# A graph layer in fp32 on one core: edge-part adds two units behind TensorE, first-layer evictions on ScalarE, a longer ring of gathered rows

## The chip, the cores and the metric

The kernel runs on one core of a Trainium2 chip. The metric is the device time of one execution in microseconds (us), the median of three runs: 2553.75 us before the change (2550.78 to 2557.36). About 0.3% is what repeated runs of this kernel can tell from no change.

TensorE (PE in the profile) multiplies matrices into PSUM; VectorE (DVE) and ScalarE (ACT) read PSUM and work on SBUF; GpSimd (POOL) here issues the gathers; SyncE (SP) issues most other transfers. Each of the engines works through its own instructions in program order and waits for the others by semaphores.

## The reference, cut to what matters

There are 6250 nodes with 256 features, and 206250 edges sorted by destination, each with a polarity and 64 raw features.

```python
h = relu(layernorm(x))
e = relu(raw @ W_e1.T + b_e1) @ W_e2.T + b_e2        # first and second layer, per edge
edge_emb = (e * (polarity + 0.01)) @ W_le.T + b_le
msg = relu(h[src] + edge_emb)
aggr = segment_sum(msg, dst)                          # sums over the edges of a node
n = layernorm((h + aggr) @ W_g1.T + b_g1) * ln_g + ln_b
out = x + relu(n) @ W_g2.T + b_g2
```

## The kernel before

**Tiling.** Edges are cut into 403 blocks of 512 (a block is four tiles of 128 edges). A *unit* is half a block, 256 edges; there are 806. A *pair* is two blocks, that is four units; its raw features come in one load (`load_pair`, line 232). W_e2 and W_le are multiplied together once (line 383), so that an edge needs two matrix products: the *first layer* (line 237) and the *edge part* (line 264). Six blocks make a *group*, whose sums gather in a PSUM accumulator.

**The steps of one unit and pair.**
- `first_layer(q)`, for a pair: four matmuls (line 248) into four PSUM buffers, then four evictions with bias and relu into `e1`: three by ScalarE (line 257) and the fourth by VectorE (line 254).
- `edge_part(u)`: four matmuls (line 272) of `e1` with the joint matrix into one PSUM buffer `pz`, then one VectorE add of the bias row, `msg = pz + bc_s` (line 277), which empties the buffer. (ScalarE copies a few of the first 22 instead, line 275.)
- gather: GpSimd fetches the 256 rows `h[src]` by two indirect DMAs (line 537) into `hg`, a ring of HG = 16 units.
- `whole(u)`: two VectorE operations (line 584) make `hg = msg * polarity + hg`, then ScalarE applies relu in place (line 589).
- `add_up(b)`: sixteen-fold narrow matmuls (line 601) sum the rows of a block into the group's accumulator by a selection matrix that VectorE builds (line 566).
- The nodes of 128-wide windows are finished in steps spread over later units (`finish_nodes`, line 148, and `node_work`, line 649); VectorE's parts that read TensorE's results are at lines 175, 197 and 703.

**What sets the order.** The order is written out by hand: the program runs in the order in which Python issues it (`manual_schedule`), each engine in its own queue. The main loop (line 750) runs over units. `forward(u)` issues the edge part; when u % 4 is 1 it calls `turn_of`. For pairs 6 to 195 (`by_two`), a *turn* comes every eight units and issues two first layers with the sums between them (lines 298 to 302). There are 95 such turns. After `forward`, the loop issues a piece of selection or node work, then `whole` for units that lie a distance behind (line 758): 22 units at first, one less every 36 units, at least LEAST = 1. Then it issues a node step that is due (not in the loop's passes 0 and 1 of eight).

**Buffers.** `pz`, the first layer's results and the nodes' products share one rotation of seven PSUM buffers (line 224); the eighth holds the group accumulators. A buffer is reused by the seventh allocation after its own, as soon as its reader is done. Gathers are issued in step with TensorE and never further ahead than HG units past the last sums (line 553).

Of the kernel before, what the change touches and what calls it, by code (L numbers as in the profile page):

```python
# [9 lines left out]
F32 = mybir.dt.float32  # L10
I32 = mybir.dt.int32
AF = mybir.ActivationFunctionType
# [5 lines left out]
P = 128  # L18
N = 6250
D = 256  # L20
# [16 lines left out]
NP = -(-NB // 2)  # L37
MARGIN = 768
DEG = E // N
LEAD = 22  # L40
LEAST = 1
# [1 line left out]
STEP = 1.282  # L43
AFLOAT = 6.0
SHRINK = 36
HG = 16
FEW = 6
QUIET = (0, 1)
TURN = 1
# [47 lines left out]
def gnn_kernel(ctx: ExitStack, tc: tile.TileContext, x, src_c, dst_c, dst_r, pol_c, raw_t, w_e1t, w_e2,  # L97
               w_let, w_g1t, w_g2t, vec_c, row_v, x_t, out):
    nc = tc.nc
# [20 lines left out]
    bc_s = const.tile([P, 2, D], F32, name="bc_s")  # L120
# [96 lines left out]
    with fast:  # L217
# [19 lines left out]
        def first_layer(q):  # L237

            bs = [b for b in (2 * q, 2 * q + 1) if b < NB]
            if not bs:  # L240
                return
            for b in bs:
                e1[b] = e1_p.tile([P, 2, 512], F32, name="e1")
            pe = {}
            for c in range(2):
                for s, b in enumerate(bs):
                    pe[s, c] = ps().rearrange("p a b -> p (a b)")
                    z = nc.tensor.matmul(pe[s, c], we1_s[s * F:(s + 1) * F, c * P:(c + 1) * P],  # L248
                                         raw[q][s * F:(s + 1) * F, :], start=True, stop=True)
                paced(LAYER, z)  # L250
            for c in range(2):
                for s, b in enumerate(bs):
                    if s == c == 1:
                        nc.vector.tensor_scalar(e1[b][:, c, :], pe[s, c], be1_s[:, c:c + 1], 0.0, op0=ALU.add,  # L254
                                                op1=ALU.max)
                    else:
                        nc.scalar.activation(e1[b][:, c, :], pe[s, c], AF.Relu, bias=be1_s[:, c:c + 1])  # L257
            raw.pop(q)

        def plain(u):  # L260

            return u < LEAD and u % 3 == 1

        def edge_part(u):

            nonlocal last_z
            b, v = divmod(u, 2)
            pz = ps()
            for i in range(2):
                k = (2 * v + i) * P  # L270
                for c in range(2):
                    last_z = nc.tensor.matmul(pz[:, i, :], e1[b][:, c, k:k + P], wc_s[:, c, :], start=c == 0, stop=c == 1)  # L272
            msg[u] = msg_p.tile([P, 2, D], F32, name="msg")
            if plain(u):
                nc.scalar.activation(msg[u], pz, AF.Copy)
            else:
                nc.vector.tensor_add(msg[u], pz, bc_s)  # L277
            if v == 1:
                e1.pop(b)
            paced(EDGE, last_z)  # L280

        last_z = None
        sums = lambda last: None
        paced = lambda us, behind: None

        def by_two(q):
            return FEW <= q < NP - FEW

        def turn_of(q):


            if not by_two(q):
                if q + 2 < NP:
                    first_layer(q + 2)
                sums(q == NP - 1)
                load_pair(q + 4)
            elif q % 2 == 0:
                first_layer(q + 2)
                sums(False)
                first_layer(q + 3)  # L300
                load_pair(q + 4)
                load_pair(q + 5)
# [39 lines left out]
        with tc.tile_pool(name="p1", bufs=4) as p1, tc.tile_pool(name="p1x", bufs=11) as p1x:  # L342
# [76 lines left out]
            for k in range(len(parts) + 1):  # L419
# [15 lines left out]
                for _ in range((k > 0) + (k > 2 and k % 3 > 0)):  # L435
                    u = next(units, None)
# [85 lines left out]
        with tc.tile_pool(name="hg", bufs=HG) as hg_p, tc.tile_pool(name="ms", bufs=5) as ms_p, \  # L522
# [227 lines left out]
            for u in range(LEAD, NU):  # L750
# [219 lines left out]
```

## Time and profile before

| | |
|---|---|
| median of 3 runs | 2553.75 us |
| the profiled execution | 2558.52 us |
| its span, first to last instruction | 2556.8 us |
| mean granted TensorE clock | 0.965 |
| TensorE busy | 2378.9 us, 93% |
| VectorE busy | 1647.0 us, 64% |
| ScalarE busy | 980.9 us, 38% |
| GpSimd busy | 1638.7 us, 64% |

The profile is of one execution. Busy time counts an engine's own work, not its waits. A row of a group has the line, engine, operation, what it writes and reads with its shape, and the count; after the first bar its busy time in us and the mean of one in ns; after the second the idle time of the engine just in front of those instructions, with what ended most of it. The chain of work that ended last goes back from the last instruction, at each step to whatever released it. A timeline row has start and duration in us, and in brackets the idle time before it. Ends of matmuls are modelled. PE is TensorE's matmuls, PEld its weight loads. A stretch's row has the length, then the busy time of PE, PEld, DVE, ACT and POOL with counts, then the granted clock, the DMA share and GB/s.

### The profile page before, as it was taken

How to read it: one execution, taken by the hardware profiler on the slowest of the kernel's cores; microseconds unless marked ns; L12 is line 12 of the kernel's file. 1: busy time of each engine (PE TensorE's matmuls, PEld its weight loads, DVE VectorE, ACT ScalarE, POOL GpSimd, SP SyncE). 2: the span in 40 equal slices, each digit the busy share in tenths (PEclk: the TensorE clock that was granted, in tenths of full speed). 3: DMA queues.
4: the chain of work that ended last, by engine and by line, in shares of the span. 5: the costliest groups of instructions: out<-in, count | busy, mean ns of one | idle time of the engine just before them, and what ended most of it. 6: DMA issues, size and time to landing. Idle time of an engine off the chain costs nothing.

```text
span 2556.8 us, 35901 instructions
## 1 busy us (share of the span) xinstructions
PE 2378.9 (93%) x12382; PEld 1670.3 (65%) x12382; DVE 1647.0 (64%) x3953; ACT 980.9 (38%) x1701; POOL 1638.7 (64%) x1675
## 2 busy tenths in 40 slices
PE   9998998999999989999999999999999999899987
PEld 7666666666666757666666666666666666666664
DVE  7776666666666666666656666656666666656655
ACT  7333333343343433334333433433333433333432
POOL 5666666666666666666666666666666665666662
PEclk9999999999999999998999999999999999999998
DMA  8433343334334433433343444334334333343341
GB/s 300 129 115 113 108 134 112 114 114 130 113 108 125 130 119 106 133 108 117 111 144 101 115 126 122 110 106 137 112 114 131 118 107 114 109 131 109 119 119 55
DMA packets 156084, 309.24 MB, mean 121 GB/s; under 512 B 33183, under 2 KB 77944, under 8 KB 155896
## 3 DMA queue, kind: packets, MB, share of 16 engines
q0 software_dynamic: 77376, 211.39, 28.5%
q1 hardware_dynamic: 77364, 92.23, 11.4%
q10 hardware_dynamic: 1156, 3.28, 0.3%
q8 instruction: 98, 1.61, 0.3%
q14 instruction: 90, 0.74, 0.1%
HBM read 293.92 MB, written 12.85 MB: 120 GB/s over the span
## 4 chain that ended last, share of the span: by engine, by line
PE 82%; issue 5%; DVE 5%; another core or an unknown queue 3%; ACT 1%; DVEq 0%; ACTq 0%
PE pz L272 49%; PE pz L248 17%; PE pd L601 9%; PE pz L701 3%; DVE hg L584 2%; PE pz L195 2%; PE pz L169 2%; DVE msg L277 1%; ACT e L257 0%; DVE sel L566 0%; PE pz L185 0%; ACT hg L589 0%; DVE hT L676 0%; DVE e L254 0%
## 5 line engine op out<-in xcount | busy, mean ns | idle before, releaser
L537 POOL DMA_INDIRECT hg<-hb_d,src_s x1612 | 1601.5, 993 | 861.2 <-issue 525.4
L272 PE MATMUL pz<-wc_s,e 128*128 128x256 f32 x6448 | 1486.5, 384 | 51.8 <-issue 38.6
L272 PEld LDWEIGHTS pz<-wc_s,e 128*128 128x128 f32 x6448 | 1216.7, 192 | 318.8 <-issue 99.8
L589 ACT ACTIVATE hg<-hg 128x512 f32<-128x512 f32 x805 | 508.5, 632 | 1117.2 <-DVE hg L584 854.1
L277 DVE TENSOR_TENSOR msg<-pz,bc_s 128x512 f32<-128x512 f32 x799 | 546.6, 686 | 325.1 <-PE pz L272 152.3
L584 DVE SCALAR_TENSOR_TENSOR hg<-msg,pol_s,hg 128x256 f32<-128x256 f32 x1612 | 697.5, 480 | 2.6 <-issue 1.5
L248 PE MATMUL pz<-raw,we_s 64*128 64x512 f32 x1612 | 510.3, 653 | 42.8 <-issue 22.9
L254 DVE TENSOR_SCALAR e<-pz,vecs 128x512 f32<-128x512 f32 x201 | 150.5, 749 | 500.0 <-PE pz L248 201.4
L257 ACT ACTIVATE e<-pz,vecs 128x512 f32<-128x512 f32 x605 | 376.4, 686 | 225.1 <-PE pz L248 84.9
L248 PEld LDWEIGHTS pz<-raw,we_s 64*128 64x128 f32 x1612 | 177.2, 195 | 281.6 <-issue 164.7
L601 PE MATMUL pd<-hg,sel 128*32 128x256 f32 x3216 | 258.6, 408 | 53.1 <-issue 50.9
L601 PEld LDWEIGHTS pd<-hg,sel 128*32 128x32 f32 x3216 | 114.0, 115 | 221.2 <-issue 170.0
L566 DVE SCALAR_TENSOR_TENSOR sel<-iota_w,zero_c,rel 128x128 f32<-128x128 f32 x403 | 138.8, 344 | 0.0
L613 ACT ACTIVATE ms<-pd 128x256 f32<-128x256 f32 x66 | 25.5, 386 | 191.7 <-remote 60.1
L701 PEld LDWEIGHTS pz<-s,ms 128*128 128x128 f32 x548 | 70.3, 194 | 9.1 <-issue 3.8
L701 PE MATMUL pz<-s,ms 128*128 128x128 f32 x548 | 71.7, 278 | 4.7 <-issue 2.5
L676 DVE SCALAR_TENSOR_TENSOR hT<-hT,zero_c,stb 128x128 f32<-128x128 f32 (+1 forms) x196 | 67.2, 343 | 1.7 <-issue 1.7
L169 PE MATMUL pz<-wg_s,hT 128*128 128x256 f32 (+1 forms) x196 | 52.8, 389 | 9.9 <-DVE hT L703 7.4
L195 PE MATMUL pz<-wg_s,nT 128*128 128x256 f32 (+1 forms) x196 | 53.9, 393 | 5.6 <-ACT hg L589 2.7
L169 PEld LDWEIGHTS pz<-wg_s,hT 128*128 128x128 f32 (+1 forms) x196 | 36.5, 191 | 20.0 <-DVE hT L703 9.7
L379 POOL TENSOR_TENSOR hb<-xt,rows_b 128x256 f32<-128x256 f32 (+1 forms) x49 | 34.2, 729 | 23.4 <-DMA xt<-in_x_dram 12.7
L195 PEld LDWEIGHTS pz<-wg_s,nT 128*128 128x128 f32 (+1 forms) x196 | 37.7, 195 | 15.2 <-issue 6.4
(91 smaller groups left out, 393.0 us busy)
## 6 DMA issues: line engine op xcount, KB each, us to landing
raw<-in_raw_t_dram SPq DMA_DIRECT2D x202, 256.0 KB
hg<-hb_d,src_s POOLq DMA_INDIRECT x1612
stb<-st_d SPq DMA_DIRECT2D x49, 128.0 KB
hb_d<-hb SPq DMA_DIRECT2D x12, 512.0 KB
xt<-in_x_dram SPq DMA_DIRECT2D x48, 128.0 KB
hT<-in_x_t_dram SPq DMA_DIRECT2D x48, 128.0 KB
out_dram<-ot SPq DMA_DIRECT2D x48, 128.0 KB
xt<-in_x_dram SPq DMA_DIRECT2D x11, 512.0 KB
```

Source lines behind the costliest of these rows:

```text
L169: nc.tensor.matmul(ph[:n, 0, :], aT[:, c, :n], wg1_s[:, c, :], start=c == 0 and not bias_by_pe, stop=c == 1)
L195: nc.tensor.matmul(po[:n, 0, :], nT[:, c, :n], wg2_s[:, c, :], start=c == 0, stop=c == 1)
L248: z = nc.tensor.matmul(pe[s, c], we1_s[s * F:(s + 1) * F, c * P:(c + 1) * P], raw[q][s * F:(s + 1) * F, :], start=True, stop=True)
L254: nc.vector.tensor_scalar(e1[b][:, c, :], pe[s, c], be1_s[:, c:c + 1], 0.0, op0=ALU.add, op1=ALU.max)
L257: nc.scalar.activation(e1[b][:, c, :], pe[s, c], AF.Relu, bias=be1_s[:, c:c + 1])
L272: last_z = nc.tensor.matmul(pz[:, i, :], e1[b][:, c, k:k + P], wc_s[:, c, :], start=c == 0, stop=c == 1)
L277: nc.vector.tensor_add(msg[u], pz, bc_s)
L537: g = nc.gpsimd.indirect_dma_start(out=hg[u][:, i, :], out_offset=None, in_=hb_d, in_offset=bass.IndirectOffsetOnAxis(ap=src_s[:, 2 * u + ...
L584: nc.vector.scalar_tensor_tensor(hg[u][:, i, :], m[:, i, :], pol_s[:, 2 * u + i:2 * u + i + 1], hg[u][:, i, :], op0=ALU.mult, op1=ALU.add)
L589: nc.scalar.activation(hg[u], hg[u], AF.Relu)
L601: z = nc.tensor.matmul(acc[g][j * W:(j + 1) * W, :], sel[g][:, k * S + j, :], m[:, j % 2, :], start=k == 0, stop=b == blocks_of(g)[-1])
L701: nc.tensor.matmul(pa[:, c, :n], ms[g][:, c * P:(c + 1) * P], box["sel2"][i][:, :n], start=i == 0, stop=i == len(gs) - 1)
```

## The change

- For the pairs 6 to 195 all four evictions of a first layer go to ScalarE (line 257); line 254 is left for the pairs at the start and the end.
- Between those pairs the add of a unit is no longer issued with its matmuls. `edge_part` puts the buffer into `parts_of`; the new function `added(behind)` issues adds until only `behind` are left. The loop calls `added(2)` after `whole`, and the turn calls `added(0)` after the sums, ahead of the second first layer. Elsewhere the add still follows its unit.
- The least distance of `whole` is 3 units instead of 1 between those pairs.
- HG is 20 instead of 16.
- The memory that the program reserves in each SBUF partition for the descriptors of GpSimd's DMAs is set to 8192 bytes; without the argument it is 16384. Four units of `hg` take 8192 bytes of a partition.

The instructions of TensorE, GpSimd and SyncE keep their order. ScalarE has 190 more and VectorE 190 fewer.

```diff
-HG = 16
+HG = 20
+BEHIND = 2
...
-                    if s == c == 1:
+                    if s == c == 1 and not (FEW <= q < NP - FEW):
                         nc.vector.tensor_scalar(e1[b][:, c, :], pe[s, c], be1_s[:, c:c + 1], 0.0, op0=ALU.add,
                                                 op1=ALU.max)
                     else:
...
-            msg[u] = msg_p.tile([P, 2, D], F32, name="msg")
-            if plain(u):
-                nc.scalar.activation(msg[u], pz, AF.Copy)
-            else:
-                nc.vector.tensor_add(msg[u], pz, bc_s)
+            parts_of[u] = pz
             if v == 1:
                 e1.pop(b)
             paced(EDGE, last_z)
+            if not by_two(u // 4):
+                added(0)
+
+        def added(behind):
+
+            while len(parts_of) > behind:
+                u = next(iter(parts_of))
+                pz = parts_of.pop(u)
+                msg[u] = msg_p.tile([P, 2, D], F32, name="msg")
+                if plain(u):
+                    nc.scalar.activation(msg[u], pz, AF.Copy)
+                else:
+                    nc.vector.tensor_add(msg[u], pz, bc_s)
...
             elif q % 2 == 0:
                 first_layer(q + 2)
                 sums(False)
+                added(0)
                 first_layer(q + 3)
...
                 piece()
-                while made < u + 1 - max(LEAST, LEAD - u // SHRINK) - (by_two(u // 4) and (u + 1) % 8 == TURN):
+                least = LEAST + BEHIND * by_two(u // 4)
+                while made < u + 1 - max(least, LEAD - u // SHRINK) - (by_two(u // 4) and (u + 1) % 8 == TURN):
                     gathers(made + 1)
                     whole(made)
                     made += 1
+                added(BEHIND)
                 due()
...
-    nc = bacc.Bacc("TRN2", target_bir_lowering=False, num_devices=1)
+    nc = bacc.Bacc("TRN2", target_bir_lowering=False, num_devices=1, dynamic_dma_scratch_size=8192)
```

More of the change, by code (lines that the diff above doesn't have):

```diff
@@ L280, in edge_part @@
             paced(EDGE, last_z)
+            if not by_two(u // 4):
[9 more added lines that the diff above has]
+                    nc.vector.tensor_add(msg[u], pz, bc_s)
+        parts_of = {}
         last_z = None
```

## The prediction

> **What bounds the kernel now.** The page comes first: its head, the chain of work that ended last (by engine), and the groups.
>
> ```profile
> span 2556.8 us, 35901 instructions
> ...
> PE 2378.9 (93%) x12382; PEld 1670.3 (65%) x12382; DVE 1647.0 (64%) x3953; ACT 980.9 (38%) x1701; POOL 1638.7 (64%) x1675
> ...
> PE 82%; issue 5%; DVE 5%; another core or an unknown queue 3%; ACT 1%; DVEq 0%; ACTq 0%
> ...
> L537 POOL DMA_INDIRECT hg<-hb_d,src_s x1612 | 1601.5, 993 | 861.2 <-issue 525.4
> L272 PE MATMUL pz<-wc_s,e 128*128 128x256 f32 x6448 | 1486.5, 384 | 51.8 <-issue 38.6
> ...
> L589 ACT ACTIVATE hg<-hg 128x512 f32<-128x512 f32 x805 | 508.5, 632 | 1117.2 <-DVE hg L584 854.1
> L277 DVE TENSOR_TENSOR msg<-pz,bc_s 128x512 f32<-128x512 f32 x799 | 546.6, 686 | 325.1 <-PE pz L272 152.3
> L584 DVE SCALAR_TENSOR_TENSOR hg<-msg,pol_s,hg 128x256 f32<-128x256 f32 x1612 | 697.5, 480 | 2.6 <-issue 1.5
> ...
> L254 DVE TENSOR_SCALAR e<-pz,vecs 128x512 f32<-128x512 f32 x201 | 150.5, 749 | 500.0 <-PE pz L248 201.4
> L257 ACT ACTIVATE e<-pz,vecs 128x512 f32<-128x512 f32 x605 | 376.4, 686 | 225.1 <-PE pz L248 84.9
> ```
>
> TensorE is the bound: 93% busy, 82% of the chain. What it does not hold of the chain is what a reordering can win. VectorE is busy only 64%, yet it idles 325.1 us in front of the add L277 and 500.0 us in front of the eviction L254, both waiting for TensorE. It works in program order, so whatever stands behind such a wait is late, although the engine has time. TensorE then waits for two things that VectorE feeds: the rows L584 (through L589) that the sums L601 read, and the PSUM buffers that L277 empties.
>
> Where in the run does this cost? The chain of waits, taken in four stretches (shares of each stretch):
>
> ```profile
> by line: PE pz L272 48.1%; PE pz L248 15.0%; PE pd L601 7.4%; issue 6.5%; DVE hg L584 3.5%; another core or an unknown queue 2.8%; DVE msg L277 2.4%; PE pz L701 2.1%; PE pz L195 1.5%; PE pz L169 1.4%; ACT e L257 1.0%; DVE sel L566 0.9%; ACT
> ...
> by line: PE pz L272 53.2%; PE pz L248 18.7%; PE pd L601 9.4%; issue 4.5%; PE pz L701 3.0%; another core or an unknown queue 2.4%; PE pz L195 1.8%; PE pz L169 1.8%; DVE hg L584 1.6%; DVE msg L277 1.5%; ACT e L257 0.4%; PE pz L185 0.4%; DVE s
> ...
> by line: PE pz L272 53.9%; PE pz L248 17.8%; PE pd L601 10.6%; issue 5.0%; PE pz L701 2.8%; PE pz L195 2.2%; DVE hg L584 2.0%; PE pz L169 1.8%; DVE msg L277 1.3%; another core or an unknown queue 0.4%; DVE sel L566 0.4%; ACT e L257 0.3%; PE
> ...
> by line: PE pz L272 54.9%; PE pz L248 19.3%; PE pd L601 10.5%; issue 5.2%; PE pz L701 2.6%; PE pz L195 2.2%; another core or an unknown queue 2.0%; PE pz L169 1.8%; PE pz L185 0.4%; DVE hg L584 0.3%; DVE msg L277 0.3%; DVE hT L703 0.2%; ACT
> ```
>
> They are 100 to 700, 700 to 1300, 1300 to 1900 and 1900 to 2460 us. DVE and ACT entries make 7.8%, 3.5%, 4.0% and 0.8%: 46.8 + 21.0 + 24.0 + 4.5 = **96 us**. "Unknown" (waits whose releaser the profile doesn't find) makes 2.8%, 2.4%, 0.4% and 2.0%: 16.8 + 14.4 + 2.4 + 11.2 = **45 us**. These 141 us are what I divide below.
>
> How a turn (line 298 to 302: first layer, sums, first layer) loses them, from the timeline of one:
>
> ```profile
> 1500.98 1.99 PE L248 MATMUL pz<-raw,we_s 64*128 64x512 f32 x8
> ...
> 1502.90 2.95 PE L601 MATMUL pd<-hg,sel 128*32 128x256 f32 x32
> ...
> 1503.60 0.69 DVE L277 TENSOR_TENSOR msg<-pz,bc_s 128x512 f32<-128x512 f32 x1 [0.62 <-PE pz L248]
> ...
> 1505.78 2.21 PE L248 MATMUL pz<-raw,we_s 64*128 64x512 f32 x8
> ...
> 1506.12 0.69 DVE L277 TENSOR_TENSOR msg<-pz,bc_s 128x512 f32<-128x512 f32 x1
> ...
> 1506.71 0.74 DVE L254 TENSOR_SCALAR e<-pz,vecs 128x512 f32<-128x512 f32 x1
> ...
> 1511.36 0.75 DVE L254 TENSOR_SCALAR e<-pz,vecs 128x512 f32<-128x512 f32 x1 [3.90 <-PE pz L272]
> ...
> 1512.29 1.67 DVE L584 SCALAR_TENSOR_TENSOR hg<-msg,pol_s,hg 128x256 f32<-128x256 f32 x4
> ...
> 1513.87 0.69 DVE L277 TENSOR_TENSOR msg<-pz,bc_s 128x512 f32<-128x512 f32 x1
> ```
>
> Against that, the chain's rows of a turn without a stall:
>
> ```profile
> 1203.44 1.92 PE pz L248 x8
> 1205.36 1.86 PE pd L601 x32
> 1207.22 1.92 PE pz L248 x8
> 1209.14 3.65 PE pz L272 x16
> ```
>
> The stalled turn takes 2.88 us from sums to second first layer instead of 1.86, since the three adds before the first L254 end only at 1506.8. VectorE then does nothing for 3.90 us until the second L254 is released; its four L584 and the next period's first add follow from 1512.29 on. Also to be seen: the L248 matmuls that this L254 reads were over at 1507.99, and it starts at 1511.36. The signal from TensorE came some 3 us after the recorded matmul. Every wait for TensorE in VectorE's queue is exposed to such lateness.
>
> **The change part by part.**
>
> *First-layer evictions to ScalarE.* Pairs 6 to 195: 190 of the 201 L254. VectorE loses 190 x 0.749 = 142 us of work and the waits before them (190/201 of 500.0 = 473 us). ScalarE gains 190 x 0.686 = 130 us, 38% to 43% busy, beside TensorE's work. I cost it at nothing: the cover is the rotation of seven PSUM buffers. Counted in allocations, the first layer's four go on to the next first layer's fourth matmul and then to the next three units. The fourth eviction, now last of four at 0.686, ends 2.7 us after the first begins, some 4 us after the layer does. Its buffer is wanted by the third unit after the turn; by the clean turn above that unit starts 5.70 us (the turn) + 3.65 us (two units) = 9.35 us after the layer began. If the cover were gone it costs 0.686 each: 130 us. Behind these evictions on ScalarE wait the L589 of the next rows, not wanted before the next turn.
>
> *Adds two units behind.* 799 adds stay as many and as long. Within a period VectorE now does the rows (L584) and selections of unit u first and then the add of u-2, whose signal has had two units (3.5 us) more to arrive. The order of TensorE, GpSimd and SyncE is unchanged, DMAs included; on the other two nothing but these adds, the 190 evictions and what they are moved past changes place. What the add now stands behind is one unit's L584 pair (0.96 us) and a selection (0.34).
>
> *Flush in the turn.* Three adds (2.06 us) stand behind the sums in the program, and the second first layer's buffers 1 to 3 wait for them. By the clean turn that layer begins 3.78 us after the turn does. After the flush VectorE is free at once: its first L584 comes about 5 us earlier than at 1512.29. What is late next: node steps (L175, L197, L703) that read TensorE's newest results, three per node window; there VectorE waits for TensorE's head instead of lagging behind it.
>
> *Least distance 1 + 2.* Differs only from unit 720 to 783; at 784 two rows' worth of L584 (1.9 us) must be caught up. Plus 2 us.
>
> *Ring of 20, and half of the memory for gather descriptors (8192).* L584 idled 2.6 us in 1612: gathers were never late, so the ring wins nothing, but it holds the earlier L584 harmless. What the smaller descriptor memory costs no row shows. Below: nothing. Above: POOL idles 861.2 us before 1612 gathers, so 0.53 us more for each would still be hidden, and beyond that it shows one to one. I take zero, the row it is nearest to being the idle time; the upper end is 20 us.
>
> *Sum.* Of the 96 us I take three quarters (72): the turn's waits and the lag that they make go, the node steps' waits stay. Of the 45 us I take a third (15), since a buffer still can't be emptied before its signal comes. -72 - 15 + 2 = **-85 us**. The profiled execution took 2558.5 (span 2556.8 and 1.7 around it), 4.8 above the median 2553.75. 2558.5 - 85 = 2473.5, against the median **2469 us**. All 141 us gone would be 2413.
>
> **Rivals.**
>
> *The clock follows.* Behind a long stall the trace shows the granted clock fall:
>
> ```profile
> 552.30:557.30 5.00, 1.99 (x7) 0.60 (x7) 0.77 (x2) 2.10 (x4) 3.78 (x5) 1.00 0.34 98
> 557.30:564.10 6.80, 5.82 (x12) 2.91 (x13) 1.52 (x3) 2.34 (x4) 2.58 (x4) 0.50 0.23 65
> ...
> 94.00:2460.00 2366.00, 2212.08 (x11571) 1551.78 (x11571) 1525.91 (x3621) 895.73 (x1535) 1537.55 (x1551) 0.97 0.40 118
> ```
>
> Mean clock 0.97 over 2366 us costs 71 us. Without the stalls half of it (35) might go too: 96 + 30 + 35 gone is 2393. Against it: in such stretches TensorE mostly waits for "issue", nothing that another engine does, and its instructions stay as they are. The Trainium skill, "TensorE: Matmul & The Clock Gate" (What's actually happening), says that an idle window of about 3.4 us halves TensorE's clock; the trace agrees (1.99 of 5.00 us busy, then 0.50 for 6.8 us). Chance 0.08.
>
> *Late signals take the place.* VectorE goes on waiting for TensorE, at node steps and at the flush; only the lag of the turn's 3.90 us is won, and a quarter of the 96 us with it: 2553.75 - 24 = 2530. For it: 325.1 us of idle time before adds. Chance 0.14.
>
> *Buffers held (slower).* If VectorE still comes late to the flush, buffers that were given back one add at a time now come back behind one more add and one more selection: 0.69 + 0.34 = 1.03 us in each of 95 turns, 98 us if in all, about 50 if in half: 2604. It decides where VectorE starts its three adds later than 3.78 - 2.06 = 1.7 us after the turn begins; in the stalled turn it did (1503.60 - 1500.98 = 2.6). Against it: VectorE loses 142 us of work and 473 us of blocking. Chance 0.12.
>
> *ScalarE alone is too slow (slower).* All 130 us land on the path: -87 + 130 = +43, 2597. It needs ScalarE some 5 us late in the turn. Against it: its waits are for VectorE (854.1 us before L589), which comes earlier. The Trainium skill, "TensorEngine Tiling (Array Packing)" (PSUM Bottleneck), advises to use both ScalarE and VectorE to empty PSUM, which speaks against this part; the rows give ScalarE the time (38% busy). Chance 0.10.
>
> *It doesn't do what it says* (VectorE's adds wait as long as now): no change, 0.02.
>
> **How the numbers follow.** Forecast 0.54: 2469, own range 2420 to 2520. Measurement tells about 0.3% (8 us) from no change. Faster: 0.54 + 0.08 and two thirds of the late-signal case, 0.71; same 0.07; slower 0.22. The range runs from 2388 (clock) to 2585, which leaves out the upper part of the two slower cases (about 0.14) and some 0.04 below.
>
> **What would show it.** L254 should fall to 11 on VectorE, L257 rise to 795 with TensorE's waits for it no larger; VectorE's idle time before adds should fall below 100 us, L703 and L175 gain idle time; the DVE entries of the chain should fall below 1.5%. Turns should show 1.92, 1.86, 1.92 more often. It is wrong if TensorE's L248 wait longer for adds than now, if L584 begins to wait for gathers, or if the halved descriptor memory lengthens the 993 ns.

## The result, and the profile after

The changed kernel takes 2580.72 us (median of 4 runs, 2571.64 to 2590.39) against 2552.77 us for the kernel before beside it (4 runs): a ratio of 1.0096, 95% interval 1.0069 to 1.0123 (as recorded, from all the runs; the two medians alone give 1.0109). It is **slower by 1%**, where 2469 us was forecast. The profiled execution took 2575.12 us, 16.6 more than that of before; the medians are 28 apart. Both profiled executions have a mean granted clock of 0.965, so the clock has no part in these 16.6 us. Over its four runs the changed kernel has 0.956 to 0.965.

The page of the changed kernel: head, the chain by engine, and the groups that answer to those of before (a line is now one higher up to L273, then 12 or 13 higher: the adds L277 are L290, the rows L584 are L596, the relu L589 is L601, the sums L601 are L613).

```profile
span 2573.2 us, 35919 instructions
...
PE 2391.3 (93%) x12382; PEld 1676.4 (65%) x12382; DVE 1535.4 (60%) x3763; ACT 1060.6 (41%) x1891; POOL 1669.9 (65%) x1675
...
PE 82%; issue 6%; DVE 6%; another core or an unknown queue 2%; DMA 1%; ACT 1%; POOL 0%; POOLq 0%; ACTq 0%; DVEq 0%
...
L549 POOL DMA_INDIRECT hg<-hb_d,src_s x1612 | 1632.6, 1013 | 838.4 <-issue 485.5
...
L596 DVE SCALAR_TENSOR_TENSOR hg<-msg,pol_s,hg 128x256 f32<-128x256 f32 x1612 | 707.4, 479 | 160.6 <-DMA hg<-hb_d,src_s 136.0
L601 ACT ACTIVATE hg<-hg 128x512 f32<-128x512 f32 x805 | 476.2, 637 | 617.0 <-DVE hg L596 458.1
L258 ACT ACTIVATE e<-pz,vecs 128x512 f32<-128x512 f32 x795 | 495.0, 689 | 555.3 <-PE pz L249 196.3
L290 DVE TENSOR_TENSOR msg<-pz,bc_s 128x512 f32<-128x512 f32 x799 | 526.7, 683 | 178.9 <-PE pz L273 84.3
...
L715 DVE SCALAR_TENSOR_TENSOR hT<-hT,pz 128x256 f32<-128x256 f32 x48 | 20.2, 421 | 229.3 <-PE pz L713 101.0
...
L198 DVE TENSOR_TENSOR ot<-pz,xt 128x256 f32<-128x256 f32 (+1 forms) x49 | 20.7, 422 | 142.6 <-PE pz L196 78.6
L176 DVE TENSOR_TENSOR hs<-pz,rows_b 128x256 f32<-128x256 f32 x47 | 19.9, 423 | 142.1 <-PE pz L273 75.2
```

The forecast moves of work came: ScalarE has 795 evictions, VectorE is busy 60% instead of 64%, the adds wait 178.9 us instead of 325.1 (the prediction asked for under 100), and the 500.0 us in front of the evictions are all but gone from VectorE. But its waits have moved, not gone. The node steps L715, L198 and L176 now stand idle 229.3 + 142.6 + 142.1 = 514 us, where the groups of before have for the same three:

```profile
L197 DVE TENSOR_TENSOR ot<-pz,xt 128x256 f32<-128x256 f32 (+1 forms) x49 | 20.6, 420 | 7.6 <-remote 4.2 <-PE pz L195 2.3 <-PE pz L272 1.2
L703 DVE SCALAR_TENSOR_TENSOR hT<-hT,pz 128x256 f32<-128x256 f32 x48 | 20.1, 419 | 31.6 <-PE pz L272 14.6 <-remote 14.1 <-PE pz L195 2.7
L175 DVE TENSOR_TENSOR hs<-pz,rows_b 128x256 f32<-128x256 f32 x47 | 19.7, 419 | 3.6 <-PE pz L248 3.6
```

31.6 + 7.6 + 3.6 = 43 us. And the rows L596, which never waited, now wait 160.6 us, 136.0 of it for gathers. The chain in the four stretches of the prediction (100 to 700, 700 to 1300, 1300 to 1900, 1900 to 2460 us):

```profile
by line: PE pz L273 53.1%; PE pz L249 18.7%; PE pd L613 9.9%; issue 6.5%; PE pz L713 2.2%; DMA hg<-hb_d,src_s 1.9%; PE pz L170 1.5%; PE pz L196 1.3%; DVE msg L290 1.3%; DVE hg L596 0.9%; ACT e L258 0.3%; PE pz L186 0.3%; POOL hg L549 0.3%; 
by line: PE pz L273 52.9%; PE pz L249 17.1%; PE pd L613 9.7%; issue 6.1%; another core or an unknown queue 2.6%; PE pz L713 2.4%; PE pz L196 1.8%; PE pz L170 1.5%; DVE hg L596 1.2%; DVE msg L290 1.1%; ACT e L258 0.9%; DMA hg<-hb_d,src_s 0.7
by line: PE pz L273 46.8%; PE pz L249 17.4%; PE pd L613 10.6%; issue 6.2%; another core or an unknown queue 3.7%; DVE hg L596 3.3%; DVE msg L290 1.9%; PE pz L713 1.9%; PE pz L196 1.4%; PE pz L170 1.2%; DMA hg<-hb_d,src_s 0.9%; POOL hg L549 
by line: PE pz L273 53.3%; PE pz L249 17.6%; PE pd L613 9.5%; issue 6.0%; another core or an unknown queue 2.7%; PE pz L713 2.5%; PE pz L170 1.6%; DVE hg L596 1.6%; PE pz L196 1.5%; DVE msg L290 1.4%; DMA hg<-hb_d,src_s 0.5%; PE pz L186 0.4
```

Summed as in the prediction, DVE and ACT entries are 15.0 + 19.2 + 31.2 + 16.8 = 82 us where they were 96: 14 won instead of 72. The gathers now have 24 us of the chain (11.4 + 4.2 + 5.4 + 2.8), "unknown" 53 instead of 45, and "issue", TensorE waiting for nothing that the profile shows, 146 us (39.0 + 36.6 + 37.2 + 33.6) instead of 125 (39.0 + 27.0 + 30.0 + 29.1). This last row, which the prediction had set aside, is as large as the loss. So are the gathers' 24 us, but a run below (after_early) takes their waits away and wins nothing. These are sums of one execution of each kernel.

From the first turn's start to the last's it is 2361.1 us before and 2378.6 after, 17.5 more, so the 16.4 us of span are lost among the turns and not at the beginning or the end. By parts of a turn (means over 93, from the first layer's start): up to the sums 2.54 us before and 2.64 after, the sums 3.17 and 3.45, the second first layer 2.71 and 2.68, the rest 16.74 and 16.56. What grew most is the sums, by 0.28 us a turn or 26 us in all; the medians of the three parts went from 1.92, 1.98, 2.19 to 1.92, 2.73, 1.92.

### The profile page after: what moved, and what is told of

Read it like the earlier page. It is cut to its first block, busy times and chain, and to the rows that moved or that the text cites. A ratio compares the mean times of both kernels' runs of the same rounds, so it can differ in the third digit from the quotient of the medians.

```text
span 2573.2 us, 35919 instructions
## 1 busy us (share of the span) xinstructions
PE 2391.3 (93%) x12382; PEld 1676.4 (65%) x12382; DVE 1535.4 (60%) x3763; ACT 1060.6 (41%) x1891; POOL 1669.9 (65%) x1675
## 4 chain that ended last, share of the span: by engine, by line
PE 82%; issue 6%; DVE 6%; another core or an unknown queue 2%; DMA 1%; ACT 1%; POOL 0%; POOLq 0%; ACTq 0%; DVEq 0%
PE pz L273 50%; PE pz L249 17%; PE pd L613 9%; PE pz L713 2%; DVE hg L596 2%; DVE msg L290 2%; PE pz L196 2%; PE pz L170 1%; DMA hg<-hb_d,src_s 1%; DVE sel L578 0%; ACT e L258 0%; DVE st L141 0%; POOL hg L549 0%; PE pz L186 0%
## 5 line engine op out<-in xcount | busy, mean ns | idle before, releaser
L549 POOL DMA_INDIRECT hg<-hb_d,src_s x1612 | 1632.6, 1013 | 838.4 <-issue 485.5
L273 PE MATMUL pz<-wc_s,e 128*128 128x256 f32 x6448 | 1499.5, 387 | 42.4 <-issue 30.4
L273 PEld LDWEIGHTS pz<-wc_s,e 128*128 128x128 f32 x6448 | 1228.4, 193 | 318.2 <-issue 96.3
L596 DVE SCALAR_TENSOR_TENSOR hg<-msg,pol_s,hg 128x256 f32<-128x256 f32 x1612 | 707.4, 479 | 160.6 <-DMA hg<-hb_d,src_s 136.0
L601 ACT ACTIVATE hg<-hg 128x512 f32<-128x512 f32 x805 | 476.2, 637 | 617.0 <-DVE hg L596 458.1
L258 ACT ACTIVATE e<-pz,vecs 128x512 f32<-128x512 f32 x795 | 495.0, 689 | 555.3 <-PE pz L249 196.3
L290 DVE TENSOR_TENSOR msg<-pz,bc_s 128x512 f32<-128x512 f32 x799 | 526.7, 683 | 178.9 <-PE pz L273 84.3
L613 PE MATMUL pd<-hg,sel 128*32 128x256 f32 x3216 | 270.4, 396 | 76.1 <-issue 70.9
L613 PEld LDWEIGHTS pd<-hg,sel 128*32 128x32 f32 x3216 | 114.5, 112 | 254.6 <-issue 208.3
L715 DVE SCALAR_TENSOR_TENSOR hT<-hT,pz 128x256 f32<-128x256 f32 x48 | 20.2, 421 | 229.3 <-PE pz L713 101.0
L198 DVE TENSOR_TENSOR ot<-pz,xt 128x256 f32<-128x256 f32 (+1 forms) x49 | 20.7, 422 | 142.6 <-PE pz L196 78.6
L176 DVE TENSOR_TENSOR hs<-pz,rows_b 128x256 f32<-128x256 f32 x47 | 19.9, 423 | 142.1 <-PE pz L273 75.2
L391 POOL TENSOR_TENSOR hb<-xt,rows_b 128x256 f32<-128x256 f32 (+1 forms) x49 | 34.2, 731 | 24.4 <-ACT xt L387 16.8
```

The source lines that it names most:

```text
L549: g = nc.gpsimd.indirect_dma_start(out=hg[u][:, i, :], out_offset=None, in_=hb_d, in_offset=bass.IndirectOffsetOnAxis(ap=src_s[:, 2 * u + ...
L596: nc.vector.scalar_tensor_tensor(hg[u][:, i, :], m[:, i, :], pol_s[:, 2 * u + i:2 * u + i + 1], hg[u][:, i, :], op0=ALU.mult, op1=ALU.add)
L601: nc.scalar.activation(hg[u], hg[u], AF.Relu)
L613: z = nc.tensor.matmul(acc[g][j * W:(j + 1) * W, :], sel[g][:, k * S + j, :], m[:, j % 2, :], start=k == 0, stop=b == blocks_of(g)[-1])
```

## What a stall looks like

This timeline is of the kernel with the adds delayed alone (adds_only, below), where the pattern is plainest: TensorE first, then ScalarE and VectorE, then the stretches with their granted clock.

```profile
1292.96 1.99 PE L249 MATMUL pz<-raw,we_s 64*128 64x512 f32 x8
1294.88 1.71 PE L613 MATMUL pd<-hg,sel 128*32 128x256 f32 x20
1297.60 0.38 PE L613 MATMUL pd<-hg,sel 128*32 128x256 f32 x1 [1.01 <-issue]
1298.31 0.39 PE L613 MATMUL pd<-hg,sel 128*32 128x256 f32 x1 [0.34 <-issue]
1299.01 0.39 PE L613 MATMUL pd<-hg,sel 128*32 128x256 f32 x1 [0.31 <-issue]
1299.72 0.38 PE L613 MATMUL pd<-hg,sel 128*32 128x256 f32 x1 [0.32 <-issue]
...
1304.48 4.31 PE L249 MATMUL pz<-raw,we_s 64*128 64x512 f32 x8
1308.72 1.99 PE L273 MATMUL pz<-wc_s,e 128*128 128x256 f32 x8
```

```profile
1301.12 1.26 ACT L258 ACTIVATE e<-pz,vecs 128x512 f32<-128x512 f32 x2 [9.31 <-remote]
```

```profile
1292.19 0.68 DVE L290 TENSOR_TENSOR msg<-pz,bc_s 128x512 f32<-128x512 f32 x1
1303.26 0.75 DVE L255 TENSOR_SCALAR e<-pz,vecs 128x512 f32<-128x512 f32 x1 [10.39 <-remote]
```

```profile
1293.00:1301.00 8.00, 5.12 (x33) 1.72 (x32) 0.00 (x0) 0.00 (x0) 5.19 (x6) 1.00 0.74 228
1301.00:1312.00 11.00, 9.91 (x31) 5.14 (x32) 5.72 (x12) 5.19 (x9) 5.63 (x7) 0.69 0.42 119
```

The first layer's matmuls are recorded at 1292.96 to 1294.9, and the first eviction starts on ScalarE at 1301.1, that on VectorE at 1303.3: both do nothing for 8 us (busy 0.00). TensorE itself gets on with twenty matmuls of the sums and then with one matmul and its weight load per 0.70 us. From 1301 to 1312 the granted clock is 0.69 on average: half for 6.8 of these 11 us. From the start of the turn to its next edge part it takes 5.70 us in the clean turn of the prediction; here it takes 15.76 (1292.96 to 1308.72). I call it a **stall** where five or more TensorE instructions, weight loads counted, start over 0.55 us after the one before them, each within some 2.3 us of the last such start, and counted them in the timelines: 21 before and 27 after in the profiled executions. The count is of one execution and hangs on this rule by a few, so a difference of five or so says little. By turns between 200 and 2450 us: before, 62 turns without a stall or half clock take 23.77 us on average and 27 others 28.53; after, 57 take 23.67 and 31 take 28.42.

## The experiments

At first four theories stood: the halved descriptor memory makes gathers late; VectorE asks for rows earlier than the gathers are paced; ScalarE alone is too slow; the delayed adds are the loss. Ratios are against the kernel before on the same chip, with the 95% interval; "stalls" are of one profiled execution; "half clock" is (1 - granted clock) x span, median of all runs, and beside it that of before on the same chip. It is the time that half clock costs if TensorE is busy throughout, and so an upper estimate.

| kernel | ratio | interval | stalls | half clock, us (before) |
|---|---|---|---|---|
| mem_only | 0.9995 | 0.9977 to 1.0012 | 19 | 76 (76) |
| evict_only | 1.0037 | 1.0020 to 1.0055 | 21 | 89 (76) |
| adds_only | 1.0241 | 1.0206 to 1.0276 | 31 | 117 (76) |
| no_ring | 1.0140 | 1.0113 to 1.0166 | 18 | 89 (76) |
| behind0 | 1.0033 | 1.0009 to 1.0058 | 26 | 90 (89) |
| behind1 | 1.0107 | 1.0069 to 1.0144 | 31 | 102 (78) |
| flush_first | 1.0189 | 1.0170 to 1.0209 | 32 | 131 (90) |
| after_b0 | 1.0007 | 0.9989 to 1.0025 | 19 | 76 (78) |
| after_early | 1.0111 | 1.0081 to 1.0142 | 23 | 93 (78) |
| pause_before | 1.0154 | 1.0114 to 1.0195 | 18 | 98 (89) |
| pause_adds | 1.0448 | 1.0410 to 1.0486 | 40 | 139 (89) |
| pause_after | 1.0222 | 1.0178 to 1.0266 | 24 | 116 (89) |
| spread_before | 0.9976 | 0.9964 to 0.9989 | 12 | 54 (90) |
| spread_adds | 1.0252 | 1.0227 to 1.0276 | 24 | 126 (90) |
| spread_after | 1.0020 | 0.9999 to 1.0040 | 18 | 78 (90) |
| spread_b0 | 0.9965 | 0.9946 to 0.9984 | 15 | 63 (78) |
| paced_adds | 1.0112 | 1.0096 to 1.0127 | 0 | see below |
| paced_after | 1.0074 | 1.0060 to 1.0088 | 0 | see below |

### The parts one by one

**mem_only**, the kernel before with the smaller descriptor memory:

```diff
-    nc = bacc.Bacc("TRN2", target_bir_lowering=False, num_devices=1)
+    nc = bacc.Bacc("TRN2", target_bir_lowering=False, num_devices=1, dynamic_dma_scratch_size=8192)
```

> The kernel before with 8192 bytes of descriptor memory in place of 16384, and nothing else. Descriptor-memory theory (gathers became late because half as many descriptors can stand ready): slower by 20 to 45 us, the mean gather goes from 993 to 1010 ns or more, and the idle time before the rows' operation (2.6 us before) rises to over 30 us. Early-demand theory (gathers are late because VectorE now asks for them sooner): within 8 us of before, gather at 993 ns, idle time under 5 us.

0.9995, a mean gather of 992 ns and 0.9 us of idle time before the rows. The memory costs nothing; its theory falls.

**evict_only**, the evictions of pairs 6 to 195 on ScalarE alone:

```diff
-                    if s == c == 1:
+                    if s == c == 1 and not (FEW <= q < NP - FEW):
```

> The kernel before with all four first-layer evictions of pairs 6 to 195 on ScalarE, and nothing else. ScalarE theory (the relus of the rows stand behind evictions that wait for TensorE, so the sums are late): slower by 20 us or more, with more idle time of TensorE before the sums. My prediction's step (an eviction less on VectorE takes its waits away): faster by 20 to 60 us. Adds theory (the loss is in the adds): faster too.

1.0037: 9 us of loss, neither the 20 us of one theory nor the gain of the other. VectorE's 470 us of waits before its evictions turned into waits before the adds (830.8 us instead of 326.2 in mem_only), at nearly the same time. That idle time was not a price.

```profile
L277 DVE TENSOR_TENSOR msg<-pz,bc_s 128x512 f32<-128x512 f32 x799 | 547.4, 687 | 830.8 <-PE pz L272 503.9
```

**adds_only**, BEHIND = 2 with the flush and the least distance as in the change, the evictions, HG = 16 and the descriptor memory as before; and **no_ring**, the change without HG = 20 and the descriptor memory, whose edit this is (against the change):

```diff
-HG = 20
+HG = 16
...
-    nc = bacc.Bacc("TRN2", target_bir_lowering=False, num_devices=1, dynamic_dma_scratch_size=8192)
+    nc = bacc.Bacc("TRN2", target_bir_lowering=False, num_devices=1)
```

> The kernel before with the adds two units behind, the flush in the turn and the least distance of 3; the fourth eviction stays on VectorE, ring 16 and descriptor memory 16384 as before. Adds theory (buffers are held until a later point of VectorE's program): slower by 20 to 50 us and more idle time of TensorE before the edge part's and the first layer's matmuls. Descriptor-memory theory and ScalarE theory: faster by 10 to 60 us.

> The kernel after with ring 16 and descriptor memory 16384 as before, so adds and evictions changed alone. Descriptor-memory theory: faster than before by 20 to 80 us, and the idle time before the rows' operation falls from 160.6 us to under 20. Early-demand theory: that idle time stays over 100 us, and the time stays within 10 us of the kernel after (2581). Adds or ScalarE theory: still slower than before by 20 us.

The delayed adds alone cost 2.4%, more than the whole change; the evictions on ScalarE win 1.0 of that back. But the reason given for it, TensorE waiting for the adds to empty buffers, is all but absent. TensorE's waits in mem_only (as good as the kernel before) and in adds_only (us in total, times, longest):

```profile
PE pd L601 <- issue: 50.3, 88, 1.5
...
PE pz L248 <- issue: 16.6, 30, 1.7
PE pz L248 <- DVE msg L277: 16.1, 18, 2.5
```

```profile
PE pd L613 <- issue: 67.7, 103, 1.7
PE pz L249 <- issue: 42.4, 54, 4.1
PE pz L249 <- DVE msg L290: 15.8, 12, 2.1
```

Waits for adds stay at 16 us (in front of the first layer's weight loads they even fall, from 55.0 to 15.1); "issue" rises from 50.3 to 67.7 in the sums and from 16.6 to 42.4 in the first layer. The turns without stall or half clock even gain (23.62 us in mem_only, 23.10 here), but the others are 39 instead of 23, at 28.6 instead of 28.3 us: 16 x 5 us = 80 lost, 49 x 0.5 = 25 won, against 62 us measured. Of these 62, the half clock alone has up to 117 - 76 = 41. By parts of a turn, as above, adds_only is longer than mem_only in all three parts of the turn (2.90, 3.67 and 3.00 us against 2.52, 3.24 and 2.71) and shorter in the rest (16.00 against 16.43).

Stalls and half clock are not the whole of it: no_ring has no more stalls (18) and 13 us more of half clock, and is 37 us slower. In its trace the time from the first layer's start to the sums is 3.16 us a turn, where mem_only has 2.52; that is 60 us in all. The sums add 20, and the second first layer and the rest give back 57. One part of the 60 is seen: TensorE waits there for buffers that node steps hold.

```profile
PE pz L249 <- ACT nT L189: 8.7, 4, 4.1
PE pz L249 <- DVE ot L198: 6.9, 3, 3.7
```

Such waits of the first layer for these two steps are in all seven profiles with the adds two units behind and the sums in one piece on these chips (from 5.8 us in the change and 6.8 in adds_only to 29.6 in pause_after), and in none of the seven with less delay, behind1 among them. So the delay does bring waits for held buffers, by way of node steps, but they are a small part of the loss, and behind1 loses 1.1% without them. The rest of no_ring's loss isn't found.

### Which property of the delayed adds

**behind0** and **behind1** are adds_only with

```diff
-BEHIND = 2
+BEHIND = 0
```

or 1, which sets the least distance with it (1 or 2 units); with 0 the add still stands behind the rows of its period, but none is left over. **flush_first** is adds_only with the flush ahead of the turn:

```diff
+                added(0)
                 first_layer(q + 2)
                 sums(False)
-                added(0)
                 first_layer(q + 3)
```

> As the kernel with the adds behind, but with none left over: the add of a unit still stands behind the rows and the selection of its period, but no longer two units later, so nothing is flushed in the turn but the unit just made, and the least distance is 1. Buffer theory, flush: if the three adds in the turn cost, this is at most half as slow as that kernel, 1.000 to 1.012 of before. If it is the place behind the rows, it is as slow, 1.02 or more. Issue-stall theory: between, with the number of stalls deciding (5 us each).

> As the kernel with the adds two units behind (ring 16, eviction on VectorE), but one unit behind, least distance 2. If each unit of delay costs: about half of the way from 1.003 (none behind) to 1.024 (two behind), 1.010 to 1.017, with 28 or so stalls. If only the second unit costs (three adds in the flush in place of two): under 1.008.

> The kernel with the adds two units behind, but flushed ahead of the turn's first first layer instead of behind its sums, so that no buffer of an edge part is held through the turn. Held-buffer theory (seven buffers are full while the sums run, so any late signal stops TensorE): back to 1.000 to 1.010 of before, stalls back to about 20. If VectorE's closer following alone brings the stalls: 1.015 or more, stalls near 30.

0.3, 1.1 and 2.4% for none, one and two units: each unit of delay costs, the place behind the rows at most 0.6. Half clock goes with it: 1, 24 and 41 us more than before. flush_first, in which no edge part's buffer is held through the turn, is at 1.0189 with 32 stalls, where the theory that these held buffers are the loss asked for 1.010 or less. So they are not the main part of it; the place of the flush may have a fifth (2.4 to 1.9%), but the two intervals overlap.

**after_b0** is the change with the same line (BEHIND = 0), **after_early** the change with gathers let further ahead:

```diff
-AFLOAT = 6.0
+AFLOAT = 12.0
```

> The kernel after with nothing left behind: evictions on ScalarE, ring 20, descriptor memory 8192, each add behind the rows of its own period. If the delay of two units is the loss: 0.997 to 1.005 of before, and VectorE's wait for gathers falls from 136 us to under 40. If the loss is in the evictions and the ring together with it: 1.008 or more.

> The kernel after with the gathers let 4.7 of their steps further ahead of TensorE (the lead of 6.0 us becomes 12.0). Early-demand theory: the idle time before the rows' operation falls from 160.6 us to under 40, and the time by 10 to 30 us, to 0.998 to 1.006 of before. If those waits lie beside TensorE's own stalls and cost nothing: within 8 us of the kernel after, 1.007 or more.

Without the delay, the rest of the change (evictions, ring, descriptor memory) costs nothing that the runs can tell: 1.0007. This edit takes out the delay and the least distance that goes with it, nothing else, so the delay is the change's loss. The rows' group in after_early and in after_b0, and the adds' in after_b0:

```profile
L596 DVE SCALAR_TENSOR_TENSOR hg<-msg,pol_s,hg 128x256 f32<-128x256 f32 x1612 | 693.9, 476 | 5.8 <-DMA hg<-hb_d,src_s 4.7
```

```profile
L290 DVE TENSOR_TENSOR msg<-pz,bc_s 128x512 f32<-128x512 f32 x799 | 541.2, 685 | 716.9 <-PE pz L273 408.4
...
L596 DVE SCALAR_TENSOR_TENSOR hg<-msg,pol_s,hg 128x256 f32<-128x256 f32 x1612 | 698.6, 477 | 37.2 <-DMA hg<-hb_d,src_s 27.9
```

after_early has no wait for gathers left (4.7 us, 136.0 in the change) and is no faster (1.0111): the late rows, though on the chain, were not what held TensorE up. That they lay beside its own stalls is the likely reading; that the earlier gathers lost elsewhere what they won here is not excluded. And in after_b0 VectorE idles 716.9 us before its adds, over twice the 325.1 of the kernel before, in the same time.

### What makes a stall likely

Over six traces (before, after, mem_only, evict_only, adds_only, no_ring) gathers were busy under 60% of the 4 us ahead of the sums in 148 turns, of which 1 at most stalled at the sums; of the other 385, some 85 to 100 did, by how the rule is drawn. This goes together; that the one brings the other isn't shown. So I tried to keep gathers away from the sums. **pause_before**, **pause_adds** and **pause_after** are the three kernels in which the pacing issues none from the first layer to the sums:

```diff
                 spent += us
+                if held:
+                    return
...
+                held.append(1)
                 first_layer(q + 2)
                 sums(False)
+                held.clear()
                 first_layer(q + 3)
```

> The kernel before, in which no gather is issued behind the first layer and the sums of a turn: they follow behind the second first layer. Issue-stall theory (TensorE gets its instructions at one per 0.7 us for some turns while GpSimd's gathers run beside the sums): the turns with such a stall fall from 19 to 23 to under 10, and the time by 20 to 60 us. Buffer theory (the time is set by who empties PSUM and when): no change in the time within 10 us, or slower because rows come later.

> The kernel with the adds two units behind (ring 16, eviction on VectorE) and the same pause of the gathers. Issue-stall theory: the stalls fall from 31 to under 15, the time from 2588 to 2510 or less, since the turns without a stall are shorter with the adds behind (23.10 us against 23.62). Buffer theory: stays at 2570 to 2600.

> The kernel after with the pause. Issue-stall theory: the stalls fall from 27 to under 15 and the time is below the kernel before. Buffer theory: 1% slower than before, as the kernel after is; where the pause makes the gathers later still, more than that.

All are slower than the kernels they came from, by 1.2 to 2.0%. It was no test of the theory: the gap fell 3 to 7 us after the sums began (there gathers were busy 38 to 51% in pause_before, 58 to 61% in before), and at the sums themselves, where the stalls begin, they ran nearly as always (61 to 73% in pause_before, 65 to 71% in before).

**spread_before**, **spread_adds** and **spread_after** cut the sums into four parts (`parted` lists them, `kept` is what follows the sums) and set them between the halves of the two first layers; where adds are delayed, the flush stays between the two layers (the edit of spread_before; the function that cuts the sums is left out here):

```diff
-                first_layer(q + 2)
-                sums(False)
-                first_layer(q + 3)
+                between, kept = parted()
+                first_layer(q + 2, between)
+                first_layer(q + 3, between)
+                kept()
```

> The kernel before with the sums of a turn cut into four and set between the halves of the two first layers (two wide matmuls, sums of a block, two wide matmuls, and so on), in place of 32 narrow matmuls in a row. Density theory (the stalls, one TensorE instruction per 0.7 us, come where many short instructions follow each other): turns with such a stall fall from about 20 to under 8, and the time by 20 to 60 us. Theory of transfers (the stalls come from what the DMA engines do at that moment, whatever TensorE does): as many stalls, time within 15 us.

> The kernel with the adds two units behind (ring 16, eviction on VectorE), with the sums cut in the same way. Density theory: stalls fall from 31 to under 12 and the time from 1.024 of before to under 1.00. Theory that the held buffers themselves cost: stays at 1.015 or more.

> The kernel after with the sums cut in the same way. Density theory: from 27 stalls to under 12, and 0.97 to 0.99 of before. Otherwise 1.005 or more.

Stalls fall in all three (21 to 12, 31 to 24, 27 to 18), so the run of short instructions has a part in them, but not by as much as the density theory asked, and the delay's loss stays (spread_adds 1.0252). In spread_before the half clock falls by 36 us and only 7 are won; by this count the rest of the span grew by 29. In spread_adds the second first layer also waits for evictions, 104.6 us in 49 times, which spread_before doesn't.

**spread_b0** puts together what did not cost: the change with BEHIND = 0 and the same cut.

```diff
-BEHIND = 2
+BEHIND = 0
```

> The kernel after with nothing left behind and the sums of a turn cut in four between the halves of the first layers. If the density of narrow matmuls and the delay of the adds are the two things that count: 0.985 to 0.997 of before, faster than every kernel so far, with under 15 stalls. Otherwise 1.00 or more.

0.9965: the change without the delay and with the sums spread beats the kernel before by 0.35%. Most of that is the spread sums': spread_before alone has 0.24%, and the two intervals overlap, so no gain by the change itself is shown.

### The wait given back, on another chip

**paced_adds** and **paced_after** keep the adds two units behind, but VectorE copies one column of the newest buffer in each unit:

```diff
             if not by_two(u // 4):
                 added(0)
+            else:
+                nc.vector.tensor_copy(tick, pz[:, 1, D - 1:D])
```

> The kernel with the adds two units behind (ring 16, eviction on VectorE), and in addition VectorE copies one column of the newest unit's PSUM buffer where the add of the kernel before stood, so that it waits for TensorE once a unit as before, while the buffers are still emptied two units later. Pacing theory (VectorE no longer waits for TensorE in each unit, runs on and stands at the turn, and its work comes in bunches that hold up the gathers and the signals): back from 1.024 to 1.000 to 1.010 of before, the mean gather back from 1030 to under 1000 ns, stalls back to about 20. Held-buffer theory: stays at 1.018 or more.

> The kernel after with the same copy of one column. Pacing theory: from 1.0096 to under 1.003 of before, the mean gather under 1000 ns, VectorE's wait for gathers from 136 us to under 40. Held-buffer theory: 1.008 or more.

These two ran on a chip where the kernel before takes 2178.52 us, 14 to 15% less than on the others (2525 to 2562). The page of paced_after, and a first layer with its evictions:

```profile
span 2191.0 us, 37524 instructions
...
PE 2177.0 (99%) x12382; PEld 1612.8 (74%) x12382; DVE 1585.4 (72%) x4523; ACT 1075.6 (49%) x1891; POOL 1621.6 (74%) x1675
...
PE 96%; DMA 1%; DVE 1%; ACT 1%; issue 0%; POOL 0%; ACTq 0%; DVEq 0%
```

```profile
1199.72 1.99 PE L250 MATMUL pz<-raw,we_s 64*128 64x512 f32 x8
...
1200.94 2.42 ACT L259 ACTIVATE e<-pz,vecs 128x512 f32<-128x512 f32 x4 [1.36 <-PE pz L250]
```

TensorE is busy 99%, the granted clock is 0.997, there is not one stall, and the first layer's first eviction starts 1.2 us after the layer's first matmul in nearly every turn. In the profile of before it starts 3.6 us after it (median). Part of that is ScalarE's own lateness; but in 78 of 188 layers ScalarE stands idle ahead of this eviction, and of these 44 start over 2 us after the first matmul, up to 9.8. In paced_after none of 180 such starts is later than 1.22 us. So the stalls and the late signals are no property of the program alone. For the question asked, pacing or held buffers, this is no answer: with no stalls to lose, 1.0112 and 1.0074 can't be set beside 1.0241 and 1.0096. They do say that a delay is no gain even where signals come at once: the first layer ahead of the sums lasts 2.15 us in paced_adds and 2.02 in paced_after on average instead of 1.92, which is 22 and 10 us over 95 turns, of the 25 and 15 us lost. The 1.92 is the clean turn's: the kernel before has times but no profile on that chip. The change itself was not run there.

## Why the prediction was wrong

**The step that failed is "Of the 96 us I take three quarters (72): the turn's waits and the lag that they make go".** It took VectorE's idle time in front of adds and evictions, and the entries that went with it, as lag that a reordering wins. 14 us of the entries went where 72 were counted, and "unknown" grew by 8 where 15 were to go; the idle time moved to the node steps (43 to 514 us) and the rows. evict_only and after_b0 show that it was worth nothing: 831 and 717 us of idle time before adds, at 1.0037 and 1.0007. There is a plain reason. VectorE has 1647 us of work in a span of 2557 that TensorE sets, so some 910 us of idle time must stand somewhere, and whatever is first in line gets it. Late signals aren't needed for that: in paced_after, without a stall, VectorE still idles 606 us (2191.0 less 1585.4). The prediction itself named the node steps as "what is late next", but at no price.

The other side of the same step is "Adds two units behind", which got a later signal and no cost. Alone it costs 62 us (adds_only, 1.0241), and taking it out of the change takes the loss away (after_b0, 1.0007).

The example that the step was read from was misread too. In the stalled turn the prediction lays the 2.88 us to the three adds. But there the sums themselves are recorded at 2.95 us, and the second first layer starts at 1505.78, ahead of the third add at 1506.12 (only its later weight loads waited for an add, 0.56 us). Within the sums the weight loads waited for nothing that the profile shows:

```profile
1503.55 1.44 PEld L601 LDWEIGHTS pd<-hg,sel 128*32 128x32 f32 x27 [0.51 <-issue]
```

**"in such stretches TensorE mostly waits for "issue", nothing that another engine does, and its instructions stay as they are"** was the second error; it is the argument against the rival "the clock follows" (2393). It made the stalls a fixed amount, at best less. But they go with when the others do their work: with TensorE's program the same, the delay took half clock from 76 to 117 us (adds_only). The Trainium skill, "TensorE: Matmul & The Clock Gate" (What's actually happening), was cited for an idle window that halves the clock. The trace does not agree as the prediction said: TensorE is not idle there. In the stall above it is recorded busy 1.52 of the 3.41 us just ahead of the half clock (1298.05 to 1301.46), and in the profile of before 44% of those 3.41 us in the median of its 30 stretches of half clock, and never 0. So less than an idle window was enough.

**Point by point.** *Evictions at nothing:* nearly right; +0.4% alone, -1.0% with the delayed adds, 0.1% together with the ring and no delay. *Adds two units behind, later signal without cost:* wrong, 0.7% for the first unit and 1.3% for the second. *Flush hidden by 3.78 us of slack:* off by 0.5% at most, 2.41 less 1.89, with overlapping intervals. *Least distance, 2 us:* nothing contradicts it; it acts from unit 720 on, and the loss of adds_only over mem_only grows all along (14.5 us by the 31st turn, 38 by the 61st, 62 by the 94th). *Descriptor memory, zero:* right. *Gathers never late, ring wins nothing:* the named sign of error came (L596 waits 136.0 us for gathers), but at no price (after_early). The ring was not run alone. *Signs:* the chain's VectorE share was to fall below 1.5% and rose from 5% to 6%; clean turns were to come more often, and 57 without stall or half clock came instead of 62.

**Rivals.** "Late signals take the place" (2530, 0.14) had the mechanism of the waits right: node steps took them over. It gave the lesser gain as its end, and did not see the loss. "Buffers held" (2604, 0.12) had the sign and the place, the delayed adds, and a number near the 2580.72 measured. But its mechanism is not what the runs show: TensorE's waits for adds did not grow, and those for node steps are small. That the number is near is luck. One instance shows that such waits exist in the change:

```profile
1024.87 1.98 PE L249 MATMUL pz<-raw,we_s 64*128 64x512 f32 x6
...
1026.55 2.48 DVE L290 TENSOR_TENSOR msg<-pz,bc_s 128x512 f32<-128x512 f32 x4
1027.38 1.09 PE L249 MATMUL pz<-raw,we_s 64*128 64x512 f32 x2 [0.53 <-DVE msg L290]
```

The first layer's last matmuls wait 0.53 us for an add held back behind a node step; in the profile these sum to 11.6 us, against 15.2 before. "ScalarE alone is too slow" (2597) is refuted by evict_only (9 us, not 130) and by no_ring beside adds_only: the evictions on ScalarE win there. The outer range, 2388 to 2585, takes in the measured time only by way of these two slower rivals. That the delay is the loss is shown; by what it brings stalls and longer turns stays **open**. That VectorE works in longer bunches is argued, not shown.

## What to carry to other kernels

Idle time of an engine in front of an instruction is no measure of what moving that instruction wins. An engine with less work than the bound must idle somewhere; moving the instruction moves the wait, unless the bound engine was waiting for what stood behind it. Before a bound engine's own "issue" time and clock are set aside as fixed, see whether they differ between turns, and with what they go. Give each part of a change one kernel: here one part cost more alone than the whole change, and without it the others together cost nothing that the runs can tell.

## What the hardware showed that was not expected

- Stalls: TensorE at one matmul per 0.70 us (adds_only at 1298 us), mostly for 3 to 14 us, evictions on an idle ScalarE up to 9.8 us after a layer's first matmul (before) instead of 1.2 (paced_after), and half clock behind many of them, 12 to 40 times an execution. On one chip there are none in two profiles, and the kernel before takes 2178.52 instead of 2525 to 2562 us. What they come from no run here shows. The Trainium skill, "NOTIFIC — the notification-queue block" (Overflow: three behaviours, one of which stalls the engine), says that a full queue of trace records can hold up the engine that writes them; no run here tells whether that is at work.
- A gather's instruction takes 0.95 us (median), but 3.64 here beside VectorE's rows without a pause, and up to 4.44 in the same trace. A stretch of adds_only:

```profile
571.60 3.64 POOL L549 DMA_INDIRECT hg<-hb_d,src_s  x1 [2.10 <-PE pz L273]
571.71 0.87 DVE L596 SCALAR_TENSOR_TENSOR hg<-msg,pol_s,hg 128x256 f32<-128x256 f32 x2
572.50 0.34 DVE L211 SCALAR_TENSOR_TENSOR xt<-xt,zero_c,rows_b 128x128 f32<-128x128 f32 x1
572.76 1.66 DVE L596 SCALAR_TENSOR_TENSOR hg<-msg,pol_s,hg 128x256 f32<-128x256 f32 x4
574.34 0.68 DVE L290 TENSOR_TENSOR msg<-pz,bc_s 128x512 f32<-128x512 f32 x1
```

  Gathers over 1.5 us: 9 in before, 63 in adds_only, where VectorE makes up work in bunches; mean 993 and 1030 ns. VectorE is at its rows in 60% of the time of these 63, and in 20% of that of the gathers under 1 us. The Trainium skill, "GPSIMD Engine Reference" (Specifications), says that GpSimd shares its SBUF interfaces with VectorE and that instructions with two SBUF inputs contend; the rows L596 have two (msg and hg), and the trace agrees.
